# Edge lists of a gated graph layer: marks made by ScalarE, masked copies by GpSimd, fewer VectorE operations

## The chip, the core and the metric

The kernel runs on one core of a Trainium2 chip. The engines are PE (TensorE, with its weight loads shown as PEld), DVE (VectorE), ACT (ScalarE), POOL (GpSimd) and SP (SyncE, here only a DMA queue). The metric is device microseconds of one execution; the time of a kernel is the median of its runs.

## The reference

One layer of a graph network with a gate on every edge. `x` is 16 batches of 1024 vertices with 256 features, `adj` a 1024x1024 matrix that is nonzero in about 0.8% of its places, the diagonal among them.

```python
pre_u  = einsum('bud,dk->buk', h, W1[:d])
pre_v  = einsum('bvd,dk->bvk', h, W1[d:])
hidden = relu(pre_u[:, :, None, :] + pre_v[:, None, :, :] + b1)
S   = sigmoid(einsum('buvk,ko->buvo', hidden, W2)[..., 0] + b2[0])
a_t = einsum('buv,bud->bvd', S * A, h)
m_t = einsum('uv,bud->bvd', A, h) * h
out = beta1*h + beta2*(a_t @ Wa + ba) + beta3*(m_t @ Wm + bm)
```

Only places where `A` is nonzero count, so the kernel works on lists of edges.

## The kernel before

**Tiling.** The target vertices v are cut into 8 blocks of 128 (`NT`), the batches into 4 groups of 4 (`NG`, `GB`). A block has two halves of 64 vertices (`W`), and each half a list of up to 640 edges, that is 5 tiles (`TW`) of 128 edge slots. A block of one batch group is thus 10 steps (`T`), and the whole kernel 320 steps. The blocks 0 to 5 come first for groups 0 and 1, then 6 and 7, then all blocks for groups 2 and 3.

**A step.** POOL gathers 128 rows of 2048 numbers from a table in DRAM that holds (h W1u | h) of each source vertex, by the indices `uidx` (L528, into 8 buffers, the gather slots). PE expands the block's h W1v to the edges with a 0/1 matrix `mark` (L627, into two PSUM buffers `pc`, issued two steps ahead). DVE adds both (L657) and takes the product with W2 under the relu, for each of 4 batches (L664, four SCALAR_TENSOR_TENSOR with a sum). ACT makes the sigmoid and the gated 0/1 columns `left` (L667, L635, L671), and PE adds up the gathered h by target vertex (L680, `acc`), which makes the gather slot free again. Around them lie the table's own matmuls (L426) and the closing products of each block (L743).

**The lists.** `lists(vt)` (from L226) makes the lists of block vt. DVE turns the row of `adj` into keys, and ACT counts them (L239); DVE draws the 24 largest keys of each row (L245 and on) and how many were drawn (`used`). A product with a triangular matrix on PE (L275) and a maximum (L281) give `first`, the slot where each row's edges begin, and two operations give `held`, how many it gets. Then DVE makes the 128x640 mark: a 1 in row u at each slot from `first` to `first + held`. It is made in two passes: L294 tests slot < first + held, L301 tests slot >= first and multiplies. A small tile `R` holds for each row: held, first, the row's number times N, a one, `inw`, and the 24 keys (29 columns, `RC`). DVE multiplies it by the flags `soon` and `late` (row below 64, or not) into the two copies of `RR` (L312). POOL casts the mark to bytes (`few`, L314) and stores them with four DMAs (L317). PE multiplies mark and RR (L320, ten matmuls), so that each slot gets the values of its row; ACT copies that to `L` (L324), and DVE works out from L the slot's key, the indices `uidx` and `vidx` and the one-hot columns (L328 to L351). POOL fetches the values of `adj` by `vidx` (L360, 10 fetches per list).

**The order of the work.** Every engine runs its instructions in program order (`manual_schedule`), and the program is written in that order by generators. The lists of blocks 0 to 3 (`EARLY`) are made in the startup, in an order given by a table of strings. The lists of blocks 4 to 7 are started at steps 7, 14, 44 and 82 and have to be done by step 110. `fill` takes one piece of a list (up to the next `yield "op"`) ahead of each of the four gates L664 of a step; a `yield "slot"` or `"step"` goes on one step later, a `"wait"` two. A list with fewer DVE pieces therefore reaches each later piece in an earlier step. At step 120 POOL takes the largest remainder over all rows (L949), for a fallback that handles edges that found no slot.

Of the kernel before, what the change touches and what calls it, by code (L numbers as in the profile page):

```python
# [17 lines left out]
def kernel(  # L18
# [42 lines left out]
    nc = tc.nc  # L61
    B, N, D = x.shape
    NT = N // P
# [13 lines left out]
    RC = 5 + S  # L77
# [23 lines left out]
    def fixed(shape, name, dt=FP):  # L101
        return const.tile(shape, dt, name=name)
# [9 lines left out]
    upto = fixed([P, E], "upto")  # L112
# [7 lines left out]
    late = fixed([P, 1], "late")  # L120
    nc.vector.tensor_scalar(late, row, float(W), None, ALU.is_ge)
    soon = fixed([P, 1], "soon")
    nc.vector.tensor_scalar(soon, row, float(W), None, ALU.is_lt)


    inw = fixed([P, 1], "inw")
# [5 lines left out]
    reached = fixed([P, TW], "reached")  # L132
# [14 lines left out]

    slot, nth = fixed([P, E], "slot"), upto[:, :S]
    for j in range(TW):
        for half in range(2):  # L150
            nc.gpsimd.tensor_copy(
                slot[:, j * P + half * W:j * P + half * W + W].rearrange("p (e f g) -> p e f g", e=2, f=8),
                upto[:, j * P:(j + 1) * P].rearrange("p (e g half f) -> p half e f g", e=2, g=4, half=2)[:, half ^ j % 2])
# [11 lines left out]


    unit = fixed([P, P], "unit", FR)
    nc.vector.tensor_scalar(unit, upto[:, :P], 0.0, None, ALU.is_ge)
# [16 lines left out]
    thr = const.tile([P, NT], FP, name="thr")  # L185
    rest = const.tile([P, NT], FP, name="rest")
    nc.gpsimd.memset(val, 0.0)

# [8 lines left out]
    lst = ExitStack()  # L197
# [26 lines left out]


    def lists(vt):  # L226
        key = fetched[vt + 1][:, :N] if vt < EARLY else lst.tile([P, N], FP, name="key", bufs=1)
        (nc.sync if vt < EARLY else nc.gpsimd).dma_start(key, adjT[vt * P:(vt + 1) * P, :])
        yield "load"
        R = lst.tile([P, RC], FP, name="R", bufs=4)  # L230
        top = R[:, 5:5 + S]
        count = lst.tile([P, 1], FP, name="count", bufs=4)
        unread = whose[:, vt * NW:(vt + 1) * NW, :].rearrange("p w e -> p (w e)")[:, :N]
# [4 lines left out]
        yield "slot"  # L238
        nc.scalar.activation(unread, key, AF.Sign, accum_out=count)  # L239
        yield "cut"  # L240
# [20 lines left out]

        used = lst.tile([P, S], FP, name="used", bufs=4)
        nc.vector.tensor_scalar(used, top, 0.0, None, ALU.is_gt, ALU.add, accum_out=R[:, 0:1])
# [8 lines left out]
        nc.vector.tensor_scalar(ahead_, reached, R[:, 0:1], None, ALU.mult)  # L272
# [4 lines left out]
        first = R[:, 1:2]  # L277
        from_ = lst.tile([P, TW], FP, name="from", bufs=4)
        nc.vector.tensor_tensor(from_, pw[:, :TW], start_, ALU.add)
        yield "op"  # L280
        nc.vector.tensor_reduce(first, from_, AX.X, ALU.max)  # L281
        yield "op"

        held = lst.tile([P, 1], FP, name="held", bufs=4)
        nc.vector.tensor_scalar(held, first, -1.0, until, ALU.mult, ALU.add)
        yield "op"
        nc.vector.tensor_scalar(held, held, 0.0, R[:, 0:1], ALU.max, ALU.min)
        yield "op"
        nc.vector.tensor_tensor(R[:, 0:1], held, first, ALU.add)
        yield "op"  # L290
        nc.vector.tensor_tensor(rest[:, vt:vt + 1], count, held, ALU.subtract)
        yield "cut"
        mark = lst.tile([P, E], FP, name="made", bufs=1)
        nc.vector.tensor_scalar(mark, slot, R[:, 0:1], None, ALU.is_lt)  # L294
        yield "op"
        none = lst.tile([P, 1], FP, name="none", bufs=4)
        nc.vector.tensor_scalar(none, held, 0.0, float(N + 1), ALU.is_equal, ALU.mult)
        yield "op"
        nc.vector.tensor_scalar(held, held, -1.0, None, ALU.add)
        yield "op"  # L300
        nc.vector.scalar_tensor_tensor(mark, slot, first, mark, ALU.is_ge, ALU.mult)  # L301
        yield "op"
        last = lst.tile([P, 1], FP, name="last", bufs=4)
        nc.vector.scalar_tensor_tensor(used, nth, held, top, ALU.is_equal, ALU.mult, accum_out=last)
        yield "op"
        nc.vector.tensor_tensor(thr[:, vt:vt + 1], last, none, ALU.add)
        yield "op"
        RR = lst.tile([P, NW, RC], FP, name="RR", bufs=2)
        few = lst.tile([P, E], mybir.dt.uint8, name="few", bufs=2)
        yield "slot"  # L310
        for w, mine in enumerate((soon, late)):
            nc.vector.tensor_scalar(RR[:, w, :], R, mine, None, ALU.mult)  # L312
        yield "step"
        nc.gpsimd.tensor_copy(few, mark)  # L314
        for w in range(NW):
# [3 lines left out]
        for j in range(TW):  # L319
# [7 lines left out]
        s_of = lst.tile([P, M], FP, name="s_of", bufs=2)  # L327
        nc.vector.tensor_tensor(s_of, slot_of.rearrange("p w j -> p (w j)"), L[:, :, 1], ALU.subtract)  # L328
        yield "op"
# [3 lines left out]
        yield "op"  # L333
        nc.vector.tensor_tensor(eq, eq, L[:, :, 5:], ALU.mult)
        yield "op"
# [5 lines left out]
        yield "op"  # L341
        nc.vector.tensor_tensor(k_of, L[:, :, 2], k_of, ALU.subtract)
        yield "op"
        nc.vector.scalar_tensor_tensor(k_of, L[:, :, 3], -BIG, k_of, ALU.mult, ALU.add)
        yield "op"
        nc.vector.tensor_scalar(vidx[:, sl].rearrange("p w j -> p (w j)"), k_of, BIG + N, None, ALU.add)
        yield "op"
# [4 lines left out]
            onehot[:, sl], place.unsqueeze(1).to_broadcast([P, NW, TW, V]),  # L352
            col[:, :, :, 4:5].to_broadcast([P, NW, TW, V]), ALU.is_equal)

# [540 lines left out]
    for n in range(total + 2):  # L895
# [45 lines left out]
        if n == LISTS:  # L941
# [5 lines left out]
            nc.vector.tensor_scalar(minus[0], ident, -1.0, None, ALU.mult)  # L947
        if n == 120:
            nc.gpsimd.partition_all_reduce(longest, rest, P, bass_isa.ReduceOp.max)  # L949
            after(n + 12, count_rest)  # L950
# [115 lines left out]
```

## Time and profile before

| | |
|---|---|
| median of 3 runs | 1043.19 us (1042.17 to 1044.06) |
| profiled execution | 1040.67 us, span 1038.9 us, mean clock 0.984 |
| PE busy | 956.6 us (92%) |
| DVE busy | 965.1 us (93%) |
| ACT busy | 866.3 us (83%) |
| POOL busy | 465.6 us (45%) |

The busy time of an engine is the time in which it had an instruction of its own running; waiting, and the issue of DMAs by POOL's sequencer, are not counted apart from what their rows show. A row of the timeline gives start, duration, engine, line, operation, output and inputs. A row of the stretches gives the window, its length, the busy time of PE, PEld, DVE, ACT and POOL with the number of instructions, the mean clock that PE was granted, the busy share of the DMA engines, and GB/s.

### The profile page before, as it was taken

Reading aid. Unit: us, or ns where it says so; the run is one execution under the profiler, and the core shown is the slowest. Engines: PE = TensorE matmul, PEld = TensorE weight load, DVE = VectorE, ACT = ScalarE, POOL = GpSimd, SP = SyncE. Lnnn points to the kernel's source line nnn. Section 1 sums busy time; section 2 is a strip of 40 time slices with the busy share of each in tenths; the row PEclk is TensorE's granted clock in tenths of the full one; section 3 lists DMA queues with packets and bytes.
Section 4 is the critical chain, followed back from the end, with each engine's and each line's share of the span. In section 5 each row is a group of like instructions: output and inputs, shape, how many; then the busy total and the mean of one; then the engine's idle time right before and its main releaser. Section 6 shows DMA issues by size and latency. Waiting matters only on the chain.

```text
span 1038.9 us, 21679 instructions
## 1 busy us (share of the span) xinstructions
PE 956.6 (92%) x6393; PEld 699.2 (67%) x6393; DVE 965.1 (93%) x3388; ACT 866.3 (83%) x2722; POOL 465.6 (45%) x481
## 2 busy tenths in 40 slices
PE   7776899898888999999999899999999999999986
PEld 6653666675566766776777677777777777766753
DVE  8768999987999999999999799999999999999992
ACT  3335779787788988898999799999999999999972
POOL 4765675646256433573432333433434444444420
PEclk9878999999999999999999999999999999999999
DMA  9999999999899999999999999999999999999981
GB/s 286 336 366 363 338 354 334 342 327 384 294 338 347 348 414 362 385 367 412 407 409 404 383 412 406 390 406 403 403 373 384 380 367 361 376 375 368 378 325 34
DMA packets 133119, 375.01 MB, mean 361 GB/s; under 512 B 17680, under 2 KB 87824, under 8 KB 96784
## 3 DMA queue, kind: packets, MB, share of 16 engines
q0 software_dynamic: 50544, 301.16, 75.2%
q1 hardware_dynamic: 81824, 71.85, 21.5%
q8 instruction: 53, 0.87, 0.3%
q10 hardware_dynamic: 624, 0.52, 0.2%
q14 instruction: 74, 0.61, 0.2%
HBM read 377.53 MB, written 50.33 MB: 412 GB/s over the span
## 4 chain that ended last, share of the span: by engine, by line
PE 43%; DVE 36%; issue 10%; DMA 5%; ACT 4%; POOL 1%; another core or an unknown queue 0%; DVEq 0%; POOLq 0%; ACTq 0%
DVE fetched L664 17%; DVE fetched L657 12%; PE misc L426 12%; PE misc L743 9%; PE pc L627 8%; PE acc L680 7%; DMA fetched<-table,uidx 5%; PE misc L702 3%; DVE LT L719 2%; ACT left L671 1%; PE misc L739 1%; DVE low L489 1%; PE misc L430 1%; PE misc L777 1%; DVE cand L245 1%
## 5 line engine op out<-in xcount | busy, mean ns | idle before, releaser
L528 POOL DMA_INDIRECT fetched<-table,uidx x320 | 344.0, 1075 | 484.8 <-PE acc L680 340.0
L664 DVE SCALAR_TENSOR_TENSOR fetched<-fetched,w_b 128x256 f32<-128x256 f32 x1280 | 474.7, 415 | 0.0
L657 DVE TENSOR_TENSOR fetched<-fetched,pc 128x1024 f32<-128x1024 f32 x320 | 387.2, 1210 | 40.1 <-DMA fetched<-table,uidx 13.8
L671 ACT ACTIVATE left<-left,gt 128x16 f32<-128x16 f32 x1280 | 285.7, 298 | 0.0
L627 PE MATMUL pc<-X,mark 128*128 128x512 f32 x640 | 228.5, 451 | 33.8 <-DVE fetched L657 29.3
L680 PE MATMUL acc<-fetched,left 128*32 128x256 f32 x2560 | 186.2, 388 | 12.3 <-issue 4.9
L627 PEld LDWEIGHTS pc<-X,mark 128*128 128x128 f32 x640 | 105.8, 190 | 123.6 <-DVE fetched L657 52.7
L667 ACT ACTIVATE gt<-sc,b_b 128x4 f32<-128x4 f32 x320 | 96.8, 302 | 47.4 <-DVE fetched L664 41.2
L680 PEld LDWEIGHTS acc<-fetched,left 128*32 128x32 f32 x2560 | 73.4, 109 | 90.1 <-issue 28.0
L426 PE MATMUL misc<-w_u,hT 128*128 128x256 f32 x512 | 124.7, 391 | 6.6 <-DMA hT<-in_xT_dram 6.0
L426 PE MATMUL misc<-w_v,hT 128*128 128x256 f32 x512 | 122.6, 383 | 0.0
L743 PE MATMUL misc<-w_a,LT 128*128 128x256 f32 x496 | 117.5, 379 | 2.8 <-ACT LT L439 1.9
L743 PE MATMUL misc<-w_m,LT 128*128 128x256 f32 x496 | 118.7, 383 | 0.0
L426 PEld LDWEIGHTS misc<-w_u,hT 128*128 128x128 f32 x512 | 99.5, 196 | 24.0 <-DMA w_u<-in_W_dram 6.0
L426 PEld LDWEIGHTS misc<-w_v,hT 128*128 128x128 f32 x512 | 98.2, 192 | 15.9
L743 PEld LDWEIGHTS misc<-w_a,LT 128*128 128x128 f32 x496 | 93.8, 190 | 18.1 <-ACT LT L439 2.5
L688 ACT COPY ev<-acc 128x512 f32<-128x512 f32 x160 | 92.4, 577 | 16.2 <-PE misc L426 5.8
L635 ACT ACTIVATE left<-onehot,val 128x32 f32<-128x32 bf16 x320 | 100.1, 313 | 0.0
L360 POOL DMA_INDIRECT val<-in_adjT_dram,vidx x80 | 85.0, 1063 | 31.8 <-issue 20.8
L664 DVE DVE_READ_ACCUMULATOR fetched<-fetched,w_b 128x1 f32 x1280 | 97.8, 76 | 0.0
L743 PEld LDWEIGHTS misc<-w_m,LT 128*128 128x128 f32 x496 | 90.2, 192 | 9.9
L702 PE MATMUL misc<-ident,ev 128*128 128x128 f32 x642 | 83.2, 274 | 9.0 <-issue 3.1
(148 smaller groups left out, 885.4 us busy)
## 6 DMA issues: line engine op xcount, KB each, us to landing
hT<-in_xT_dram SPq DMA_DIRECT2D x35, 512.0 KB
table<-in_x_dram SPq DMA_DIRECT2D x32, 512.0 KB
out_dram<-z SPq DMA_DIRECT2D x62, 256.0 KB
table<-tab SPq DMA_DIRECT2D x48, 256.0 KB
fetched<-table,uidx POOLq DMA_INDIRECT x320
table<-fetched SPq DMA_DIRECT2D x8, 512.0 KB
fetched<-in_adjT_dram SPq DMA_DIRECT2D x4, 512.0 KB
key<-in_adjT_dram POOLq DMA_DIRECT2D x4, 512.0 KB
```

The costliest lines, as they stand in the source:

```text
L426: nc.tensor.matmul(p[:, bb * D:(bb + 1) * D], hT[:, 2 * h + bb, i, :], wt[:, i, :], start=(i == 0 and not begun), stop=(i == DC - 1), skip ...
L528: nc.gpsimd.indirect_dma_start(out=fetched[at_slot[n]], out_offset=None, in_=table[g], in_offset=bass.IndirectOffsetOnAxis(ap=uidx[:, vt * ...
L627: nc.tensor.matmul(pcs[n][:, c], marks[n // TW][:, j * P:(j + 1) * P], cuts[k][w][:, c], start=True, stop=True)
L635: nc.scalar.activation(lefts[n][:, 1::GB, :], onehot[:, vt * NW + w, j, :].unsqueeze(1).to_broadcast([P, GB // 2, V]), AF.Copy, scale=val[ ...
L657: nc.vector.tensor_tensor(t, t, pcs.pop(n), ALU.add)
L664: nc.vector.scalar_tensor_tensor(t[:, b, :], t[:, b, :], 0.0, w2_b, ALU.max, ALU.mult, accum_out=sc[:, b:b + 1])
L667: nc.scalar.activation(gt, sc, AF.Sigmoid, bias=b2_b)
L671: nc.scalar.activation(lefts[n][:, 2 * b, :], lefts[n][:, 1 + b // 2 * GB, :], AF.Copy, scale=gt[:, b:b + 1])
L680: nc.tensor.matmul(accs[i][b * 2 * V:(b + 1) * 2 * V, r, :], left[:, 2 * b - b % 2:2 * b - b % 2 + 2].rearrange("p k v -> p (k v)"), f[:, ...
L688: nc.scalar.copy(evs[i], accs.pop(i))
L702: nc.tensor.matmul(pt[:, :, FROM[j]:FROM[j] + V], evs[i][:, r, c * P:(c + 1) * P], ident, is_transpose=True, start=(j == of[0]), stop=True ...
L743: nc.tensor.matmul(pz[:, bb * D:(bb + 1) * D], LT[:, 2 * h + bb, i if bb else 1 - i, c, :], wt[:, c, :], start=(i == 1 and bb == 0 and c = ...
```

## The change

What it does, for each list:

- The mark is made by ACT from the distance to the middle of the row's slots. DVE writes two numbers, `span` = (held/2, −held/2 − first), and ACT computes relu(sign(held/2 − |slot + 1/2 − first − held/2|)), three dependent operations on 128x640 in place.
- The masked copies RR are made by POOL in one multiplication with a two-column tile `sides`, directly ahead of `few`. It used to be two DVE operations, a step ahead of it.
- Three columns of R (the row's number, `inw`, a constant) are the same for every list. They are written once into four tiles R, which are allocated once and used again. R has 28 columns instead of 29; the block's share of the row's number is added as a constant in the last step to `vidx`.
- `start_` is added by a second PE matmul (the identity, 128x5) into the same PSUM tile instead of by DVE.
- The threshold `thr` is one DVE operation over 25 columns of R, the first of which is the constant N + 1. It was four operations.
- ACT writes its count into `rest`, DVE leaves `held` in `taken`, and one subtraction at step 120 stands ahead of POOL's reduction.

DVE loses fourteen instructions per list and gets two. At the start, POOL writes the constant columns (4 copies) and adds 0.5 to `slot` (128x640), the latter with a switch of its library. The tile of the mark has one buffer and `few` two, as before.

The line numbers move: L320 is L314 in the changed kernel, L324 is L318, L314 is L308, L317 is L311, L528 is L520, L627 is L619, L680 is L672; new are L301 to L303 (ACT) and L306 (POOL).

On POOL, in the startup, from the first list's cast to the first gather (`val` are the value fetches, `whose` the stored marks, `fetched` a gather). Before:

```order
L314 CAST few<-made 128x640
L317 DMA whose<-few 64x640 x4
L360 DMA val<-in_adjT_dram,vidx 128x1 x10
L314 CAST few<-made 128x640
L317 DMA whose<-few 64x640 x4
L360 DMA val<-in_adjT_dram,vidx 128x1 x3
L314 CAST few<-made 128x640
L317 DMA whose<-few 64x640 x4
L528 DMA fetched_177<-table_60,uidx 128x2048
```

After, on the same engine at the same place:

```order
L306 TENSOR_TENSOR RR<-R_193,sides 128x56
L308 CAST few<-made 128x640
L311 DMA whose<-few 64x640 x4
L352 DMA val<-in_adjT_dram,vidx 128x1 x10
L306 TENSOR_TENSOR RR<-R_194,sides 128x56
L308 CAST few<-made 128x640
L311 DMA whose<-few 64x640 x4
L352 DMA val<-in_adjT_dram,vidx 128x1 x3
L306 TENSOR_TENSOR RR<-R_195,sides 128x56
L308 CAST few<-made 128x640
L311 DMA whose<-few 64x640 x4
L520 DMA fetched_182<-table_60,uidx 128x2048
```

RR now stands in POOL's queue ahead of each cast; for the second list it stands behind ten fetches, for the third behind three.

On PE, at the product of the last list, with the semaphores that an instruction waits for (Activation is ACT, DMASW a gather). Before:

```order
L680 MATMUL acc<-fetched_182,left 32x256 [waits DMASW6_49,Activation_49]
L680 MATMUL acc<-fetched_182,left 32x256 [waits Activation_49] x3
L627 MATMUL pc<-X,mark 128x512 [waits DVE_49]
L627 MATMUL pc<-X,mark 128x512
L320 MATMUL misc<-RR,made 128x58 [waits PE_49,Activation_49]
L320 MATMUL misc<-RR,made 128x58 x4
L627 MATMUL pc<-X,mark 128x512 [waits DVE_49]
```

After:

```order
L672 MATMUL acc<-fetched_185,left 32x256 [waits DMASW4_49,Activation_49]
L672 MATMUL acc<-fetched_185,left 32x256 [waits Activation_49] x3
L619 MATMUL pc<-X,mark 128x512 [waits DVE_49]
L619 MATMUL pc<-X,mark 128x512
L314 MATMUL misc<-RR,made 128x56 [waits Activation_49,Pool_49]
L314 MATMUL misc<-RR,made 128x56 x4
L619 MATMUL pc<-X,mark 128x512 [waits DVE_49]
```

The product stands at the same place among accumulates and expands, but it waits for ACT (the mark) and POOL (RR), and the expands of the next steps stand behind it.

The diff, cut to its core:

```diff
+    sides = fixed([P, NW], "sides")
+    nc.vector.tensor_scalar(sides[:, 0:1], row, float(W), None, ALU.is_lt)
+    nc.vector.tensor_scalar(sides[:, 1:2], row, float(W), None, ALU.is_ge)
...
+    nc.gpsimd.tensor_scalar(slot, slot, 0.5, None, ALU.add)
...
+    Rs = [lst.tile([P, RC], FP, name=f"R{i}") for i in range(EARLY)]
+    for R in Rs:
+        nc.gpsimd.tensor_copy(R[:, 1:4], known)
...
-        nc.vector.tensor_scalar(R[:, 2:3], row, float(N), float(vt * P * N), ALU.mult, ALU.add)
-        yield "op"
-        nc.vector.memset(R[:, 3:4], 1.0)
-        yield "op"
-        nc.vector.tensor_copy(R[:, 4:5], inw)
...
-        nc.tensor.matmul(pw[:, :TW], before, ahead_, start=True, stop=True)
+        nc.tensor.matmul(pw[:, :TW], before, ahead_, start=True, stop=False)
+        nc.tensor.matmul(pw[:, :TW], ident, start_, start=False, stop=True)
...
-        nc.vector.tensor_tensor(R[:, 0:1], held, first, ALU.add)
-        yield "op"
-        nc.vector.tensor_tensor(rest[:, vt:vt + 1], count, held, ALU.subtract)
+        nc.vector.tensor_scalar(span[:, 0:1], held, 0.5, None, ALU.mult)
+        yield "op"
+        nc.vector.scalar_tensor_tensor(span[:, 1:2], held, -0.5, first, ALU.mult, ALU.subtract)
         yield "cut"
+        nc.vector.scalar_tensor_tensor(used, upto[:, :S + 1], held, R[:, 3:], ALU.is_equal, ALU.mult,
+                                       accum_out=thr[:, vt:vt + 1])
         mark = lst.tile([P, E], FP, name="made", bufs=1)
-        nc.vector.tensor_scalar(mark, slot, R[:, 0:1], None, ALU.is_lt)
...
-        nc.vector.scalar_tensor_tensor(mark, slot, first, mark, ALU.is_ge, ALU.mult)
...
         yield "slot"
-        for w, mine in enumerate((soon, late)):
-            nc.vector.tensor_scalar(RR[:, w, :], R, mine, None, ALU.mult)
+        nc.scalar.activation(mark, slot, AF.Abs, bias=span[:, 1:2])
+        nc.scalar.activation(mark, mark, AF.Sign, bias=span[:, 0:1], scale=-1.0)
+        nc.scalar.activation(mark, mark, AF.Relu)
         yield "step"
+        RR = lst.tile([P, NW, RC], FP, name="RR", bufs=2)
+        nc.gpsimd.tensor_tensor(RR, R.unsqueeze(1).to_broadcast([P, NW, RC]), sides.unsqueeze(2).to_broadcast([P, NW, RC]),
+                                ALU.mult)
         nc.gpsimd.tensor_copy(few, mark)
...
+            nc.vector.tensor_tensor(rest, rest, taken, ALU.subtract)
             nc.gpsimd.partition_all_reduce(longest, rest, P, bass_isa.ReduceOp.max)
```

More of the change, by code (lines that the diff above doesn't have):

```diff
@@ L148 @@
     slot, nth = fixed([P, E], "slot"), upto[:, :S]
+    known = fixed([P, 3], "known")
+    nc.vector.tensor_scalar(known[:, 0:1], row, float(N), -BIG, ALU.mult, ALU.add)
+    nc.gpsimd.tensor_copy(known[:, 1:2], inw)
+    nc.gpsimd.memset(known[:, 2:3], float(N + 1))
     for j in range(TW):
@@ L276, in lists @@
+        nc.tensor.matmul(pw[:, :TW], ident, start_, start=False, stop=True)
         yield "wait"
-        first = R[:, 1:2]
-        from_ = lst.tile([P, TW], FP, name="from", bufs=4)
-        nc.vector.tensor_tensor(from_, pw[:, :TW], start_, ALU.add)
+        first = R[:, 0:1]
+        nc.vector.tensor_reduce(first, pw[:, :TW], AX.X, ALU.max)
         yield "op"
-        nc.vector.tensor_reduce(first, from_, AX.X, ALU.max)
-        yield "op"
-        held = lst.tile([P, 1], FP, name="held", bufs=4)
+        held = taken[:, vt:vt + 1]
@@ L299, in lists @@
[L299 to L308, printed above, removed]
```

41 lines of the change are left out of this document (17 added, 24 removed).

## The prediction

> **What bounds the kernel now.** I read the page first: the span, the busy time of the engines, the shares of the chain that ended last, and two groups, PE's expand and the add that takes it (busy time, mean ns, idle time ahead and what ended most of it).
>
> ```profile
> span 1038.9 us, 21679 instructions
> PE 956.6 (92%) x6393; PEld 699.2 (67%) x6393; DVE 965.1 (93%) x3388; ACT 866.3 (83%) x2722; POOL 465.6 (45%) x481
> PE 43%; DVE 36%; issue 10%; DMA 5%; ACT 4%; POOL 1%; another core or an unknown queue 0%; DVEq 0%; POOLq 0%; ACTq 0%
> L627 PE MATMUL pc<-X,mark 128*128 128x512 f32 x640 | 228.5, 451 | 33.8 <-DVE fetched L657 29.3
> L657 DVE TENSOR_TENSOR fetched<-fetched,pc 128x1024 f32<-128x1024 f32 x320 | 387.2, 1210 | 40.1 <-DMA fetched<-table,uidx 13.8
> ```
>
> TensorE and VectorE share the bound: 92% and 93% busy, 43% and 36% of the chain. The lists that the change edits are built in the startup and in some 365 us after it, so I asked for the stretches from 100 to 465 us: length, busy time of PE, PEld, DVE, ACT and POOL with their instructions, granted clock, DMA share, GB/s.
>
> ```profile
> 100.00:125.00 25.00, 20.89 (x122) 13.50 (x122) 20.85 (x80) 19.21 (x63) 16.72 (x17) 1.00 0.98 326
> 300.00:400.00 100.00, 93.84 (x624) 68.40 (x623) 95.67 (x333) 87.14 (x271) 47.11 (x48) 0.98 0.99 362
> sum 365.00, PE 333.84 PEld 241.27 DVE 340.39 ACT 304.63 POOL 196.87; mean PE 47.69 PEld 34.47 DVE 48.63 ACT 43.52 POOL 28.12
> ```
>
> In these 365 us PE is idle for 365 − 333.84 = 31.2 us and DVE for 365 − 340.39 = 24.6. Neither is full. A microsecond taken from DVE here is worth at most a microsecond, and a microsecond of PE waiting costs about as much. The question is which of the two the change moves more.
>
> **The change: what DVE loses.** Per list, fourteen DVE instructions go and two come. Their price is the distance from one instruction to the next, since on this engine they overlap. The timeline of DVE (start, duration, instruction) shows one of each kind:
>
> ```profile
> 191.53 0.15 DVE L291 TENSOR_TENSOR rest<-count,held 128x1 f32<-128x1 f32 x1
> 191.60 0.42 DVE L664 SCALAR_TENSOR_TENSOR fetched<-fetched,w_b 128x256 f32<-128x256 f32 x1
> 191.94 0.55 DVE L294 TENSOR_SCALAR made<-slot,R 128x640 f32<-128x640 f32 x1
> 192.41 0.42 DVE L664 SCALAR_TENSOR_TENSOR fetched<-fetched,w_b 128x256 f32<-128x256 f32 x1
> 195.90 0.87 DVE L301 SCALAR_TENSOR_TENSOR made<-slot,R,made 128x640 f32<-128x640 f32 x1
> 196.70 0.41 DVE L664 SCALAR_TENSOR_TENSOR fetched<-fetched,w_b 128x256 f32<-128x256 f32 x1
> 201.02 0.23 DVE L312 TENSOR_SCALAR RR<-R,soon 128x29 f32<-128x29 f32 x1
> 201.17 0.23 DVE L312 TENSOR_SCALAR RR<-R,late 128x29 f32<-128x29 f32 x1
> ```
>
> A small one costs 191.60 − 191.53 = 0.07 us, L294 0.47, L301 0.80, the two masked copies 0.15 each. Ten small ones go and two come: −8 × 0.07 = −0.56. With L294, L301 and 2 × 0.15 it is −0.56 − 0.47 − 0.80 − 0.30 = −2.13 us per list. The threshold over 25 columns for 24 is nothing I can price apart from a small one. Four lists run in the loop: −8.5. The first of them runs from about 100 us, where DVE has 20.85 of 25.00 us busy and PE 20.89, so what DVE saves there becomes waiting; I credit the other three, −6.4. The four lists of the startup are chained through other engines (below), and I credit nothing for them.
>
> **What PE gains as a wait.** The product of the marks (PE, L320 before, L314 after) used to need only what DVE had written a step earlier. Now it needs the mark from ACT and the masked copy RR from POOL, and RR stands in POOL's queue directly ahead of the cast "few", behind gathers that wait for PE itself. The best price for "when does POOL reach that place" is when it reached "few". The four products of the loop on PE, and the four casts on POOL:
>
> ```profile
> 148.15 1.22 PE L320 MATMUL misc<-RR,made 128*128 128x58 f32 x10
> 207.44 1.22 PE L320 MATMUL misc<-RR,made 128*128 128x58 f32 x10
> 297.74 1.22 PE L320 MATMUL misc<-RR,made 128*128 128x58 f32 x10
> 417.67 1.22 PE L320 MATMUL misc<-RR,made 128*128 128x58 f32 x10
> ```
>
> ```profile
> 154.57 0.90 POOL L314 CAST few<-made 128x640 uint8<-128x640 f32 x1
> 205.45 0.72 POOL L314 CAST few<-made 128x640 uint8<-128x640 f32 x1
> 300.50 0.72 POOL L314 CAST few<-made 128x640 uint8<-128x640 f32 x1
> 419.55 1.20 POOL L314 CAST few<-made 128x640 uint8<-128x640 f32 x1
> 417.04 0.99 POOL L528 DMA_INDIRECT fetched<-table,uidx  x1 [4.70 <-PE acc L680]
> ```
>
> RR itself has no row. Its nearest are a POOL copy of 128x64 and, as an upper end, the cast of 128x640; I take 0.4 us, since 56 columns lie by the first:
>
> ```profile
> L151 POOL COPY slot<-upto 128x64 f32<-128x64 f32 x10 | 2.5, 304 | 0.0
> L560 ACT CAST mark<-whose 128x640 fp32r<-128x640 uint8 x64 | 46.3, 723 | 0.0
> ```
>
> So the waits would be 154.57 + 0.4 − 148.15 = 6.8 us; none for the second list, whose cast is ahead of its product; 300.50 + 0.4 − 297.74 = 3.2; 419.55 + 0.4 − 417.67 = 2.3. Together 12.3. With fewer DVE pieces the lists finish two or three steps sooner and meet other gathers, so a single wait may move; the last gather above shows the kind of place, 4.70 us behind PE's acc. While PE stands at L314, its later expands (L619) and accumulates (L672) stand behind it, and with them DVE's adds, ACT's L318 and the gather slots.
>
> A stand of PE can cost again. Windows of 3.40 us, with the clock in the column ahead of the DMA share:
>
> ```profile
> 329.50:332.90 3.40, 1.16 (x7) 0.79 (x7) 3.40 (x11) 2.73 (x8) 2.03 (x2) 1.00 1.03 353
> 332.90:336.30 3.40, 3.40 (x10) 2.68 (x9) 2.52 (x9) 3.38 (x12) 2.48 (x4) 0.51 0.76 290
> 469.50:472.90 3.40, 1.63 (x19) 0.61 (x18) 2.98 (x11) 3.18 (x10) 2.11 (x2) 1.00 1.02 414
> 472.90:476.30 3.40, 3.40 (x20) 3.01 (x21) 3.40 (x14) 1.98 (x8) 0.37 (x1) 1.00 1.02 420
> ```
>
> With 1.16 us of work in a window, the next has half the clock (0.51), and 1.7 us of PE's work in it is lost; with 1.63 us it keeps it. A wait of about 2 us is enough, so I charge three: 3 × 1.7 = 5.1. PE then loses 12.3 + 5.1 = 17.4 us. The Trainium skill, "TensorE: Matmul & The Clock Gate", section "HAM oscillation — how this bites in real kernels", has it milder: “The abstract rule is "no PE-idle gaps >~3.4µs."” By it only the first of the waits would cost clock; the row with 1.16 of 3.40 busy, thus 2.24 us idle, and half the clock behind it, speaks against that.
>
> How much of 17.4 ends on the path? PE is 333.84/365 = 91% busy there; two pc buffers let it stand a step ahead of DVE, and eight gather slots lie between it and the transfers. Bounds are nothing and all; I take half, +8.7, as PE and DVE share the chain nearly evenly.
>
> **The rest in the loop.** ACT takes three operations of 128x640 per list, by the cast above 0.72 each, 2.2 us per list; ACT is idle 60 us of the 365 (304.63 busy), and the mark is made a step ahead of its product: nothing, or up to 2.2 where ACT's gates stand behind. PE's second matmul into the same PSUM: five columns, under 0.1. The subtract of rest and taken at step 120 is one small DVE operation; the reduction on POOL behind it then waits for DVE.
>
> **The startup.** RR of list 1 now stands behind the ten value fetches of list 0, and the product of list 1 waits for it. POOL's fetches (first and last) and its first gather, then PE's product of list 1, ACT's copy of it, DVE's first add that follows the gathers:
>
> ```profile
> 29.15 1.10 POOL L360 DMA_INDIRECT val<-in_adjT_dram,vidx  x1 [6.60 <-DVE onehot L351]
> 42.16 0.99 POOL L360 DMA_INDIRECT val<-in_adjT_dram,vidx  x1 [0.30 <-issue]
> 53.93 1.07 POOL L528 DMA_INDIRECT fetched<-table,uidx  x1 [0.33 <-issue]
> 38.29 1.22 PE L320 MATMUL pc<-RR,made 128*128 128x58 f32 x10
> 43.17 0.40 ACT L324 COPY L<-pc 128x290 f32<-128x290 f32 x1 [1.60 <-remote]
> 63.44 1.22 DVE L657 TENSOR_TENSOR fetched<-fetched,pc 128x1024 f32<-128x1024 f32 x1 [1.84 <-issue]
> 50.00:75.00 25.00, 18.99 (x70) 14.31 (x71) 16.45 (x64) 8.86 (x22) 16.72 (x21) 0.73 1.06 361
> ```
>
> The fetches end at 43.15; RR to 43.6; product to 44.8; the copy starts there and not at 43.17, 1.6 later; list 2 has its own RR on POOL, 0.4. So the first gather goes from 53.93 to about 55.9, +2.0. As the DMA engines are full in that stretch (1.06) with transfers that have to be made anyway, half of it shows: +1.0. The edits ahead of it (kept columns, slot + 0.5, and a library switch of POOL for that operation) lie in POOL's 6.60 us of waiting for DVE. The one switch of before is no dearer than the gap between these two:
>
> ```profile
> 472.96 0.37 POOL L949 PARTITION_ALL_REDUCE longest<-rest  x1 [0.21 <-issue]
> 477.55 1.03 POOL L528 DMA_INDIRECT fetched<-table,uidx  x1 [4.22 <-PE acc L680]
> ```
>
> Sum: −6.4 + 8.7 + 1.0 = +3.3 us.
>
> **The rivals.** *PE's waits are hidden* (faster). PE's expands wait 29.3 us in all for DVE's adds in the row of the expand, so PE often stands ahead of DVE; if it does so by more than some 3 us at three of the products, the waits only replace those waits. Then −6.4 + 1.0 = −5.4, 1035.3 on the profiled execution, and with the fourth list's 2.1 down to −7.5. Against it: PE was idle for only 31 us in 365, and the gather slots wait for its acc.
>
> *The clock holds* (same). If no window at the waits falls short enough, PE loses 12.3, half of it 6.2: −6.4 + 6.2 + 1.0 = +0.8. It is also what the milder rule of the Trainium skill's page would come near to: with one loss of 1.7 for three, by halves, +1.6.
>
> *The transfers decide* (same). The DMA share is 0.99 from 300 to 400 us. If gathers set the pace, DVE's saving and PE's waits both vanish into waiting for them: the startup's +1.0 is left. Against it: of 40.1 us that L657 waits, 13.8 at most are laid to a gather.
>
> *The startup slips* (slower). If PE, waiting for RR of list 1, drops to half clock, the products and the table's matmuls behind it take twice as long; PE is 18.99 of 25.00 busy there. 5 us lost at the first gather, with nothing hiding them, stand in place of 1.0: +3.3 + 4.0 = +7.3; with three quarters of 17.4 instead of half, 4.4 more, +11.7. It decides from about 5 us at the first gather.
>
> **How the numbers follow.** The profiled execution took 1040.67 us, 1.8 more than its span, and 2.5 less than the median of the three runs, 1043.2. I add the sum to the median: 1043.2 + 3.3 = 1046.5. Chances: forecast 0.32; waits hidden 0.31 (about 1037.8); clock holds 0.14 (1044.0); transfers decide 0.13 (1044.2); startup 0.10 (1050 to 1055). A measurement of this kernel can tell 0.2%, 2.1 us, from no change: faster 0.31, same 0.27, slower 0.42. The range holds the hidden waits' value at its low end and the near half of the startup's at its high end: 1037 to 1052. The forecast's own, with a quarter to three quarters of 17.4 on the path, is 1042 to 1051.
>
> **What would show it.** On PE, idle time ahead of L314 of 2 to 7 us at three of the four loop lists, released by POOL's RR; windows at half clock behind them; DVE's busy time from 100 to 465 us some 8 us lower, and its waits on pc higher; the first gather near 56. The forecast is wrong if PE hardly waits at L314 or DVE's adds don't start later behind such a wait (then faster), or if the first add comes later than 68 us.

## The result and the profile after

The changed kernel took 1057.78 us (median of 4 runs, 1051.87 to 1063.67) beside 1042.68 us for the kernel before (4 runs, 1039.82 to 1044.06): 1.0146 times the time, 95% interval 1.0104 to 1.0188. A second comparison gave 1.0114 (1.0086 to 1.0141). The sign was forecast; the size, 15 us, lies outside the range. The profiled execution took 1058.45 us.

The page of the changed kernel: span, busy time, the chain that ended last, and DVE's add.

```profile
span 1056.7 us, 21672 instructions
PE 973.5 (92%) x6409; PEld 712.4 (67%) x6409; DVE 950.4 (90%) x3294; ACT 884.6 (84%) x2746; POOL 469.0 (44%) x496
PE 53%; DVE 25%; issue 10%; ACT 5%; DMA 4%; POOL 3%; another core or an unknown queue 0%; POOLq 0%; DVEq 0%
L649 DVE TENSOR_TENSOR fetched<-fetched,pc 128x1024 f32<-128x1024 f32 x320 | 388.0, 1213 | 55.6 <-PE pc L619 29.7
```

DVE did 14.7 us less work (965.1 to 950.4), as the edit wanted, and its add waited 15.5 us longer (40.1 to 55.6); the largest part of the wait is now for PE's expand (29.7), where it was for a gather (13.8). PE's share of the chain rose from 43% to 53%, which fits a saving made on the engine that was not the tighter one.

Next, PE's first rows of the four loop products (start, duration, and in brackets the idle time ahead with its releaser), then POOL's multiplications that release them.

```profile
150.91 1.32 PE L314 MATMUL misc<-RR,made 128*128 128x56 f32 x5 [5.47 <-POOL RR L306]
207.64 1.63 PE L314 MATMUL misc<-RR,made 128*128 128x56 f32 x8 [2.87 <-POOL RR L306]
306.59 1.81 PE L314 MATMUL misc<-RR,made 128*128 128x56 f32 x9 [2.04 <-POOL RR L306]
425.58 1.58 PE L314 MATMUL misc<-RR,made 128*128 128x56 f32 x10 [1.98 <-POOL RR L306]
```

```profile
150.56 0.29 POOL L306 TENSOR_TENSOR RR<-R,sides 128x56 f32<-128x56 f32 x1
207.28 0.30 POOL L306 TENSOR_TENSOR RR<-R,sides 128x56 f32<-128x56 f32 x1
306.25 0.29 POOL L306 TENSOR_TENSOR RR<-R,sides 128x56 f32<-128x56 f32 x1
425.23 0.29 POOL L306 TENSOR_TENSOR RR<-R,sides 128x56 f32<-128x56 f32 x1
```

All four waits end some 0.35 us after RR starts. They sum to 12.36 us. RR itself takes 0.29. What it stands behind shows at the third list: two gathers, the first of which waited for PE.

```profile
303.76 0.99 POOL L520 DMA_INDIRECT fetched<-table,uidx  x1 [3.44 <-PE acc L672]
305.06 1.16 POOL L520 DMA_INDIRECT fetched<-table,uidx  x1 [0.30 <-issue]
306.25 0.29 POOL L306 TENSOR_TENSOR RR<-R,sides 128x56 f32<-128x56 f32 x1
```

The fourth list has the same picture (3.67 for PE). Ahead of the first list's RR, gathers and value fetches follow each other with 1.3 to 1.7 us from start to start, and of the last four only one waited for PE (1.35).

RR comes last, but it is not alone. ACT's mark is late as well. This is the last of its three operations at each of the four lists:

```profile
147.38 0.74 ACT L303 ACTIVATE made<-made 128x640 f32<-128x640 f32 x1
205.05 0.74 ACT L303 ACTIVATE made<-made 128x640 f32<-128x640 f32 x1
303.63 0.74 ACT L303 ACTIVATE made<-made 128x640 f32<-128x640 f32 x1
424.15 0.74 ACT L303 ACTIVATE made<-made 128x640 f32<-128x640 f32 x1
```

PE became free at 145.44, 204.77, 304.55 and 423.60 (start of the product less the wait). With RR ready it would still have waited for the mark for some 2.7, 1.0, 0 and 1.3 us: 5.0 of the 12.36. RR alone accounts for the other 7.4.

What follows the first of them shows in windows of 3.40 us (PE, PEld, DVE, ACT, POOL busy; clock; DMA share; GB/s), and in the one row of DVE behind it:

```profile
148.40:151.80 3.40, 0.89 (x4) 0.90 (x5) 3.40 (x9) 2.01 (x8) 2.78 (x4) 0.74 0.88 279
151.80:155.20 3.40, 3.40 (x12) 3.04 (x13) 0.01 (x2) 0.39 (x1) 2.19 (x4) 0.50 0.79 250
155.20:158.60 3.40, 3.40 (x13) 2.69 (x12) 0.00 (x0) 0.59 (x1) 0.00 (x0) 0.76 0.16 53
```

```profile
160.54 1.22 DVE L649 TENSOR_TENSOR fetched<-fetched,pc 128x1024 f32<-128x1024 f32 x1 [8.73 <-PE pc L619]
```

One stand of PE goes through three stages here. PE stands, the others go on. Then PE is back, but the clock is at 0.74, 0.50 and 0.76 in the three windows, together 3.4 us of it lost (some 0.4 before PE was back), while DVE and ACT have next to nothing to do. Then, as no accumulate has freed a gather slot, the DMA engines run dry, at 0.16. DVE stood 8.73 us for a wait of 5.47.

### The profile page after: what moved, and what is told of

Its sections match the earlier page's. It is cut to its first block, busy times and chain, and to the rows that moved or that the text cites. A ratio compares the mean times of both kernels' runs of the same rounds, so it can differ in the third digit from the quotient of the medians.

```text
span 1056.7 us, 21672 instructions
## 1 busy us (share of the span) xinstructions
PE 973.5 (92%) x6409; PEld 712.4 (67%) x6409; DVE 950.4 (90%) x3294; ACT 884.6 (84%) x2746; POOL 469.0 (44%) x496
## 4 chain that ended last, share of the span: by engine, by line
PE 53%; DVE 25%; issue 10%; ACT 5%; DMA 4%; POOL 3%; another core or an unknown queue 0%; POOLq 0%; DVEq 0%
PE misc L418 15%; DVE fetched L656 13%; PE misc L735 11%; PE pc L619 10%; DVE fetched L649 10%; PE acc L672 8%; PE misc L694 4%; DMA fetched<-table,uidx 2%; DMA hT<-in_xT_dram 2%; POOL fetched L520 2%; PE misc L731 2%; ACT left L663 1%; DVE LT L711 1%; PE misc L314 1%; PE misc L422 1%
## 5 line engine op out<-in xcount | busy, mean ns | idle before, releaser
L520 POOL DMA_INDIRECT fetched<-table,uidx x320 | 342.5, 1070 | 491.8 <-PE acc L672 349.3
L649 DVE TENSOR_TENSOR fetched<-fetched,pc 128x1024 f32<-128x1024 f32 x320 | 388.0, 1213 | 55.6 <-PE pc L619 29.7
L619 PE MATMUL pc<-X,mark 128*128 128x512 f32 x640 | 231.0, 455 | 22.9 <-DVE fetched L649 18.4
L672 PE MATMUL acc<-fetched,left 128*32 128x256 f32 x2560 | 187.0, 390 | 7.7 <-ACT ev L680 5.6
L619 PEld LDWEIGHTS pc<-X,mark 128*128 128x128 f32 x640 | 107.4, 192 | 112.2 <-issue 52.1
L418 PE MATMUL misc<-w_u,hT 128*128 128x256 f32 x512 | 129.1, 402 | 8.2 <-DMA hT<-in_xT_dram 5.8
L672 PEld LDWEIGHTS acc<-fetched,left 128*32 128x32 f32 x2560 | 73.1, 109 | 86.2 <-issue 24.0
L735 PE MATMUL misc<-w_a,LT 128*128 128x256 f32 x496 | 120.2, 385 | 2.3 <-ACT LT L431 1.3
L418 PEld LDWEIGHTS misc<-w_u,hT 128*128 128x128 f32 x512 | 102.5, 202 | 26.2 <-DMA w_u<-in_W_dram 5.7
L680 ACT COPY ev<-acc 128x512 f32<-128x512 f32 x160 | 92.3, 577 | 16.0 <-PE acc L672 4.9
L656 DVE DVE_READ_ACCUMULATOR fetched<-fetched,w_b 128x1 f32 x1280 | 100.7, 79 | 0.0
L627 ACT ACTIVATE left<-onehot,val 128x32 f32<-128x32 bf16 x320 | 99.9, 312 | 0.0
```

The costliest lines, as they stand in the source:

```text
L418: nc.tensor.matmul(p[:, bb * D:(bb + 1) * D], hT[:, 2 * h + bb, i, :], wt[:, i, :], start=(i == 0 and not begun), stop=(i == DC - 1), skip ...
L520: nc.gpsimd.indirect_dma_start(out=fetched[at_slot[n]], out_offset=None, in_=table[g], in_offset=bass.IndirectOffsetOnAxis(ap=uidx[:, vt * ...
L619: nc.tensor.matmul(pcs[n][:, c], marks[n // TW][:, j * P:(j + 1) * P], cuts[k][w][:, c], start=True, stop=True)
L627: nc.scalar.activation(lefts[n][:, 1::GB, :], onehot[:, vt * NW + w, j, :].unsqueeze(1).to_broadcast([P, GB // 2, V]), AF.Copy, scale=val[ ...
L649: nc.vector.tensor_tensor(t, t, pcs.pop(n), ALU.add)
L656: nc.vector.scalar_tensor_tensor(t[:, b, :], t[:, b, :], 0.0, w2_b, ALU.max, ALU.mult, accum_out=sc[:, b:b + 1])
```

## The experiments

The theory (1): RR's place in POOL's queue, behind gathers (some of which wait for PE) and value fetches, makes PE stand at the product; the half clock and the slots behind it make the loss. Rivals: (2) ACT's three operations delay its gates and copies; (3) the startup slipped. Each ratio is against the kernel before in the same comparison, whose own medians were 1037.0, 1037.4, 1025.0 and 1024.8 us in the four; so between comparisons the ratios can be compared, not the times.

**RR back on DVE.** In the changed kernel, one piece ahead of the step of the product:

```diff
+        for w in range(NW):
+            nc.vector.tensor_scalar(RR[:, w, :], R, sides[:, w:w + 1], None, ALU.mult)
         yield "step"
-        nc.gpsimd.tensor_tensor(RR, R..., sides..., ALU.mult)
```

> The changed kernel with the masked copies RR back on VectorE, one piece ahead of the step of the product; ScalarE's marks and the rest as changed. Theory 1 (PE's waits for GpSimd's RR, 12.4 us at the four loop products, make the loss): those waits go, the time falls to 1036 to 1042 us. Theory 2 (ScalarE's three operations per list delay its gates and copies): still 1052 to 1058. Theory 3 (the startup, whose first add came 3.3 us later, and what follows from it): 1050 to 1056.

1044.98 us, 1.0069 (1.0040 to 1.0099). Over half of the loss is gone, though not all that theory 1 had expected. PE's waits at the loop products fell to 2.75, 0.88, 0.83 and 1.34 us, and none is for POOL any more. The first, second and last end within 0.1 us of the end of ACT's mark (147.97, 201.82 and 412.15 in this trace).

**Marks back on DVE**, RR still on POOL:

```diff
-        nc.scalar.activation(mark, slot, AF.Abs, bias=span[:, 1:2])
-        nc.scalar.activation(mark, mark, AF.Sign, bias=span[:, 0:1], scale=-1.0)
-        nc.scalar.activation(mark, mark, AF.Relu)
+        nc.vector.tensor_scalar(mark, slot, end_, None, ALU.is_lt)
+        nc.vector.scalar_tensor_tensor(mark, slot, first, mark, ALU.is_ge, ALU.mult)
```

> The changed kernel with the marks back on VectorE (two operations on 128x640 per list), RR still on GpSimd. Theory 1: PE still waits for RR, 1055 to 1062 us. Theory 2: near the kernel before, 1040 to 1046. Theory 3: 1050 to 1058, as the library switch and GpSimd's queue of the startup are unchanged.

1058.01 us, 1.0204 (1.0149 to 1.0258). Rival 2 falls as the main cause: without ACT's marks the loss is all there. The ratio is above the changed kernel's 1.0146 and 1.0114; since these were not in one comparison, it stays open whether the marks on ACT gain something.

**Both back on DVE**, the other edits kept:

> The changed kernel with marks and RR back on VectorE; the constant columns, PE's second matmul and the one-operation threshold stay, nine VectorE operations per list fewer than before. Theories 1 and 2: 1040 to 1043 us, the kernel before or a little under. Theory 3: 1046 to 1050.

1040.44 us, 1.0031 (1.0000 to 1.0062). In time this lies in the range of theory 1; as a ratio it is a little over the kernel before, where a gain of DVE's work had been hoped for.

**RR alone on POOL**, in the kernel before:

> The kernel before with the one edit that RR is made by GpSimd, directly ahead of its cast. Theory 1: PE waits at the product as in the changed kernel, 1053 to 1060 us. Theory 2 and theory 3: within 3 us of the kernel before, 1040 to 1046.

1058.93 us, 1.0207 (1.0149 to 1.0264). One edit of 0.3 us per list makes a loss at least as large as the whole change's. It brings something else along, which is shown further down: POOL switches its library ahead of the first RR and again ahead of the reduction (9.10 and 8.49 us of idle time there in this trace). So this run does not separate the place in the queue from the switches.

**RR earlier in POOL's queue.** The same instruction, same engine, moved to right behind the maximum that completes R:

```diff
         nc.vector.tensor_reduce(first, pw[:, :TW], AX.X, ALU.max)
+        RR = lst.tile([P, NW, RC], FP, name="RR", bufs=2)
+        nc.gpsimd.tensor_tensor(RR, R..., sides..., ALU.mult)
         yield "op"
```

> The changed kernel with GpSimd's RR issued right after the maximum that completes R, so that in the loop it stands ahead of the two gathers that it stood behind; the same instruction, the same engine, only its place in GpSimd's queue. If the place in the queue is what costs (theory 1): PE's wait at the loop products falls under 1 us where the mark is ready, and the time comes near that of the kernel with RR on VectorE, 1041 to 1047 us. Rival, GpSimd's instruction itself or its sharing with VectorE costs: 1052 to 1060.

1041.18 us, 1.0033 (1.0012 to 1.0053). The library switches are still there, so the place in the queue makes most of the loss. The rival, that POOL's instruction itself costs, falls. The group of the loop's products in the changed kernel and then here (each with the last product of the startup, 3.1 and 3.9 us of the wait):

```profile
L314 PE MATMUL misc<-RR,made 128*128 128x56 f32 x50 | 10.4, 383 | 15.4 <-POOL RR L306 15.4
```

```profile
L314 PE MATMUL misc<-RR,made 128*128 128x56 f32 x50 | 8.6, 335 | 10.0 <-POOL RR L285 3.9 <-issue 3.5 <-ACT made L306 2.6
```

What POOL still releases here is the startup's; in the loop nothing waits for RR. Of the remaining 6.1 us, 5.2 end within 0.2 us of the end of ACT's mark. RR moved ahead in the startup too (the first add comes at 63.2 us, 66.7 in the changed kernel), so this run does not divide the loss between startup and loop.

**RR on POOL in the loop alone**, in the kernel before:

```diff
+        if vt < EARLY:
+            for w in range(NW):
+                nc.vector.tensor_scalar(RR[:, w, :], R, sides[:, w:w + 1], None, ALU.mult)
         yield "step"
+        if vt >= EARLY:
+            nc.gpsimd.tensor_tensor(RR, R..., sides..., ALU.mult)
```

> The kernel before with RR on GpSimd for the four lists of the loop alone; the four of the startup keep VectorE's. Theory 1 as the traces have it (the loop's waits and what follows): 14 to 20 us over the kernel before. Rival, the startup (PE idle for 3.7 and 4.0 us there, the first add 1.7 to 3.3 us later) carries a good part: 6 to 12 us over it.

1057.53 us, 1.0185 (1.0130 to 1.0240): about the number that theory 1 expected, but the run can't be read that way. POOL's rows at the first of its lists:

```profile
155.74 1.00 POOL L364 DMA_INDIRECT val<-in_adjT_dram,vidx  x1 [0.30 <-issue]
165.69 0.27 POOL L316 TENSOR_TENSOR RR<-R,sides 128x58 f32<-128x58 f32 x1 [8.95 <-issue]
```

POOL switches its library ahead of the first multiplication, for 8.95 us. In the changed kernel that switch lies in the startup; here it fell into the loop and PE stood 15.42 us at that product. The startup's share, rival 3, stays unmeasured by it. The traces tell something on it all the same. How many us later than in the kernel before the add of a step starts (steps counted from 0; one execution each, the last two columns from another comparison than the first two):

| step | kernel before | changed | rr_dve | both_dve |
|---|---|---|---|---|
| 0 | 63.44 | +3.3 | +0.3 | −0.1 |
| 20 | 138.39 | +2.8 | +3.0 | +3.3 |
| 25 | 158.14 | +10.0 | +6.0 | +1.4 |
| 50 | 241.93 | +17.4 | +7.1 | +1.7 |
| 110 | 435.42 | +12.8 | −1.4 | −2.8 |
| 319 | 1012.89 | +16.8 | +2.1 | −1.7 |

The slip of the first add by RR in the startup is no longer to be seen at step 20, where the two runs without it are as late. The changed kernel falls behind between the steps 20 and 50, with the first two products of the loop.

**PE kept busy while it would wait.** Twenty matmuls into the product's own tile, ahead of each loop product, which overwrites it:

```diff
         pe = aside(vt)
+        if vt >= EARLY:
+            for j in range(20):
+                nc.tensor.matmul(pe[:, :P], ident, before, start=True, stop=True)
```

> The changed kernel with twenty idle 128x128 matmuls on PE ahead of each of the four loop products, written into the product's own tile before it and overwritten by it (about 2.2 us of PE). If the half clock behind the waits is a large part of the loss (theory 1a): the windows at half clock at the products shrink and the time falls by 4 to 10 us against the changed kernel, 1048 to 1054. If the wait and the gather slots behind it are the loss (theory 1b): 1056 to 1063, no gain or a little loss.

1050.41 us, 1.0105 (1.0068 to 1.0143). In its own comparison there was no run of the changed kernel, and the second comparison of that, expected as follows, gave 1038.45 us, 1.0114 (1.0086 to 1.0141):

> The changed kernel itself once more, beside the versions of it on the same chip. From its first comparison, 1.0146 of the kernel before: 1.010 to 1.020, so 1048 to 1058 us where the kernel before takes 1037. If the six microseconds that the busy PE recovered are real, it stands above that run's 1.0105.

So this pair decided nothing, and it was repeated side by side further down.

**Without the slot shift on POOL.** Both back on DVE, and no library switch in the startup (`slot` stays without the half). It was run twice:

> Marks and RR on VectorE and the other edits of the change, as in the run both_dve, without the shift of the slot numbers by one half on GpSimd and its library switch. If that switch in the startup made the 3 us by which both_dve stood over the kernel before: level with the kernel before or up to 4 us under it. If not: 2 to 5 us over it, as both_dve.

> The run both_dve_plain once more with more rounds: marks and RR on VectorE, no shift, no library switch, nine VectorE operations per list fewer. If VectorE's saving of the small operations is worth its time where the loop waits for VectorE (9 times 0.07 us times 4, 2.5 us): 0.996 to 0.999 of the kernel before. If the loop's order hides it: 0.999 to 1.001.

0.9981 (0.9948 to 1.0014), then 0.9996 (0.9980 to 1.0012): no change. Nine DVE instructions fewer per list show no gain clear of noise; the 2.5 us that the prediction's price gives for four lists would be 0.9976.

**RR on DVE, marks on ACT, the shift on DVE**, so no library switch in the startup; then the same with ACT's three operations issued a step earlier:

```diff
+        nc.scalar.activation(mark, slot, AF.Abs, bias=span[:, 1:2])
+        nc.scalar.activation(mark, mark, AF.Sign, bias=span[:, 0:1], scale=-1.0)
+        nc.scalar.activation(mark, mark, AF.Relu)
         yield "slot"
-        (the same three)
```

> ScalarE's marks kept, RR on VectorE, the shift by one half on VectorE, so no library switch in the startup. If ScalarE's marks (PE waits of 2.7, 0.9, 0.8 and 1.3 us for them in the run rr_dve) are what is left of the loss: 1.004 to 1.008 of the kernel before, as rr_dve. If the library switch was: 0.998 to 1.001.

> The run rr_dve_shift_dve with ScalarE's three operations issued a step earlier, ahead of the step that they opened. If PE's waits for the mark are what is left: they fall under 0.5 us each and the time falls to 0.994 to 1.000 of the kernel before. If ScalarE's own time, in front of its gates, is the cost: no better than rr_dve_shift_dve, 1.003 to 1.008.

1.0014 (1.0000 to 1.0028) and 1.0018 (1.0008 to 1.0029). In the second, PE's products in the loop wait for 0.4 us in all:

```profile
L314 PE MATMUL misc<-RR,made 128*128 128x56 f32 x50 | 6.2, 271 | 0.4 <-ACT LT L907 0.4
```

Here DVE is spared all that the change spares it but RR, PE is not held, and the kernel is not faster than before. Taken with ACT's operations, DVE's saving is worth no time here. Whether ACT's own time eats it is not shown.

The first of these runs bears on a rival that the three theories leave out, the library switch. It differs from rr_dve in the shift alone, and 1.0069 became 1.0014. Likewise both_dve, 1.0031, became 0.9981 and 0.9996 without the switch. That is 3 to 6 us in each pair, but no pair stood in one comparison. So it is open how much of the loss, and of the 1.0033 of rr_early, is the switch's.

**The reduction moved behind the gathers.** POOL's library has to be switched again for the reduction of step 120. In the profiled execution of the changed kernel, POOL's rows of the switch in the startup and of the reduction (the kernel before had 0.21 us ahead of it):

```profile
17.22 1.84 POOL L171 TENSOR_SCALAR slot<-slot 128x640 f32<-128x640 f32 x1 [8.68 <-DVE taken L289]
...
499.16 1.42 POOL L942 PARTITION_ALL_REDUCE longest<-rest  x1 [6.76 <-issue]
```

```diff
-        if n == 120:
+        if n == 310:
...
-            after(n + 12, count_rest)
+            after(n + 6, count_rest)
```

> The changed kernel with the reduction over the rows (and the subtraction ahead of it) moved from step 120 to step 310, behind nearly all gathers. In the kernels that use GpSimd's library in the startup, 6.8 to 8.4 us stand ahead of that reduction with the gathers behind it, and steps 127 to 129 take 3 us more. If that is a real part of the loss: 3 to 6 us under the changed kernel (1.0114 and 1.0146 of the kernel before), so 1.006 to 1.009. If it is given back at step 157, where the kernel before waits 5 us for a gather: 1.011 to 1.015, as before.

1040.47 us, 1.0150 (1.0127 to 1.0173). Nothing gained. The three steps from step 127 (between DVE's adds in the trace) took 7.55 us instead of the changed kernel's 11.00, and step 160 (counted from 0, as in the table; the expectation calls the place step 157) gave it back, waiting for a gather:

```profile
579.01 1.22 DVE L649 TENSOR_TENSOR fetched<-fetched,pc 128x1024 f32<-128x1024 f32 x1 [5.78 <-DMA fetched<-table,uidx]
```

The kernel before has such a wait there too, 5.42 us; the changed kernel came late enough to have none.

The same with PE kept busy, on the same chip, and both on DVE with the reduction late:

> The run late_reduce with the twenty idle matmuls of kept_busy ahead of the four loop products. If half clock behind PE's waits is a part of the loss: 0.003 to 0.007 under late_reduce on the same chip. If only the waits and the gather slots are: level with late_reduce within 0.002.

> The run both_dve (marks and RR on VectorE, the slot shift on GpSimd with its library switch), with the reduction at step 310. If the switch costs through the reduction: from 1.003 down to 0.998 to 1.001 of the kernel before, the value without a switch. If the switch costs in the startup: still 1.002 to 1.005.

The first took 1038.77 us, 1.0126 (1.0104 to 1.0147), 1.7 us under late_reduce; the intervals overlap, and 0.0024 lies between the two values expected. The matmuls themselves took longer than meant; the stretch of the four loop lists in late_reduce, and the group of the extra matmuls and the stretch in this one:

```profile
100.00:465.00 365.00, 340.45 (x2239) 251.12 (x2239) 335.73 (x1186) 315.08 (x965) 201.50 (x201) 0.97 0.97 357
```

```profile
L315 PE MATMUL misc<-before,ident 128*128 128x128 f32 x160 | 18.6, 276 | 0.8 <-ACT low L483 0.8
```

```profile
100.00:465.00 365.00, 349.77 (x2400) 263.33 (x2392) 337.73 (x1187) 315.19 (x966) 201.64 (x201) 0.99 0.98 358
```

They held PE for 18.6 us. In late_reduce it had waited for RR in this group:

```profile
L314 PE MATMUL misc<-RR,made 128*128 128x56 f32 x50 | 9.8, 366 | 14.3 <-POOL RR L306 14.3
```

Of these 14.3 us, 3.6 belong to the last product of the startup, so 10.7 to the four of the loop. With the filler PE was held 8 us longer there, and the clock rose from 0.97 to 0.99. Added up from windows of 1 us, 12.0 us of clock are lost in that stretch without the filler and 3.4 with it, so 8.5 us came back. The time did not grow. That fits a clock that is worth about as much time as the hold: an inference from the balance, since a shorter filler was not tried. Both on DVE with the late reduction gave 1.0012 (0.9995 to 1.0028), between the values with and without the switch; it doesn't decide whether the switch costs a measurable time, and late_reduce showed no gain from moving the second one.

## Why the prediction was right in sign and wrong in size

Two terms of the sum failed. −6.4 for DVE was credited in full, and the runs show none of it. The clock behind PE's waits was charged at 5.1 us, and 12 us of it are lost. Of two things put at nothing, ACT's mark cost PE 5 us of waiting, and for the library switch it is open.

- **PE's waits: right.** Forecast 6.8, 0, 3.2 and 2.3 us, 12.3 in all; measured 5.47, 2.87, 2.04 and 1.98, 12.36. The single ones moved with the lists, as the working allowed; that the sum agrees to 0.1 us is partly luck, since the second was forecast at none. That the place in POOL's queue makes them last so long is shown by rr_early.
- **ACT's mark: put at nothing, wrong.** The working had the mark made a step ahead of its product. PE came to three of the four products before it, by 5.0 us together, and in rr_dve, where RR is ready, PE still waits for 5.8 us. Only issuing the three operations a step earlier took this away (mark_early, 0.4 us).
- **The clock: mis-sized.** The working charged one half window, 1.7 us, for each of three waits. The windows behind the first wait lose (0.26 + 0.50 + 0.24) × 3.4 = 3.4 us of clock. Over the stretch of 365 us the loss is in these rows, of the kernel before and of the changed one:

```profile
100.00:465.00 365.00, 333.84 (x2200) 241.27 (x2200) 340.39 (x1217) 304.63 (x946) 196.87 (x195) 0.99 0.98 352
```

```profile
100.00:465.00 365.00, 332.13 (x2116) 240.62 (x2116) 322.75 (x1132) 297.02 (x909) 189.47 (x192) 0.96 0.95 341
```

  0.03 × 365 = 11 us of PE, against 5.1. Windows of 1 us give it closer: 15.4 against 3.4 us, so 12.0 more, of which the four products have 3.4, 3.4, 3.4 and 1.7. The one row that showed half a clock had a single window of it, and that was taken as the length of the state. The length is not the same each time: in the second comparison's trace of the changed kernel the four products have 3.4, 1.7, 1.7 and 1.7.
- **DVE's saving of 6.4 us: failed.** It was credited in full. both_dve_again (the small operations, no gain) and mark_early (1.0018, PE's products hardly held) give nothing for it; for the mark's two operations that is shown only together with the three that ACT got in their place. It rested on "a microsecond taken from DVE here is worth at most a microsecond", and the most was taken.
- **Half of PE's loss shows: held, roughly.** With 12.4 + 12.0 = 24.4 us lost and none gained by DVE, half is 12.2. With 1 to 3 us of the startup's slip it comes to 13 to 15, and 15.1 was measured. This is a balance, not a measurement: the library switch could stand in it for the startup or for a part of PE's loss. In rr_early PE loses 6.1 us ahead of the loop's products and 5.8 us more clock than in the kernel before, and 0.0033, 3.4 us, is all that the time shows.
- **The startup: mechanism right, size low.** The first gather went to 57.39 us (forecast 55.9), and DVE's first add from 63.44 to 66.71, +3.3 where +1.0 was charged. In other runs of the same startup it came at 64.5 to 65.8, so 1 to 3 us. The ten fetches, as forecast, hold PE for 3.75 us at the product of list 1. One more cause shows in the trace: for list 2, POOL's cast waited 2.83 us for ACT's mark, and PE 3.56. At list 3 PE waited 3.07 us more for RR. How much of it reaches the end stays open; by the table above it does not show at step 20.
- **The library switch: misread.** The gap of 4.22 us behind the reduction was read as the upper end of a switch's price. It was a wait for PE; the kernel before pays no switch at that place. The two switches of the changed kernel stand ahead of their instructions, with 8.68 and 6.76 us. The first was hidden in the trace, as forecast: POOL's next cast still waited 4.19 us for ACT's mark. The second cost 11.00 − 7.54 = 3.5 us in the three steps from step 127 and was absorbed at step 160. Yet the runs with the switches stand 0.003 to 0.006 above those without, so that they cost nothing is not shown.
- **The rivals.** "PE's waits are hidden" fell: DVE's waits for the expand between 100 and 485 us (total, times, longest) grew from the kernel before to the changed one.

```profile
DVE fetched L657 <- PE pc L627: 8.0, 5, 4.6
```

```profile
DVE fetched L649 <- PE pc L619: 21.0, 10, 8.7
```

"The clock holds" fell: behind the waits of the last two products, 2.04 and 1.98 us, the changed kernel's windows show 0.50 and 0.69 of the clock.

```profile
308.80:312.20 3.40, 3.40 (x9) 2.67 (x9) 3.40 (x10) 3.40 (x13) 1.36 (x3) 0.50 0.94 366
427.80:431.20 3.40, 3.40 (x14) 2.76 (x14) 3.03 (x11) 1.34 (x7) 0.87 (x2) 0.69 1.03 416
```

The Trainium skill ("TensorE: Matmul & The Clock Gate", section "HAM oscillation — how this bites in real kernels") puts its rule at idle gaps over about 3.4 us; these gaps are shorter, so the trace does not agree. "The transfers decide" was right only at step 160, where they swallowed the reload. "The startup slips" is not shown: the first add came 3.3 us later, not 5.

No version here beat the kernel before: the best, both on DVE without the shift (0.9981 and 0.9996), is level with it.

## What to carry to other kernels

Before moving a cheap instruction to an idle engine, look at what stands ahead of it in that engine's queue and who waits for it: an operation of 0.29 us per list on GpSimd, placed behind gathers and fetches that take 1.3 us or more each and partly wait for TensorE, made most of a loss of 15 us; issued earlier in the same queue, it left a loss of 0.33%. Issue such an instruction as soon as its inputs exist, not where its result is used. Price a stand of TensorE with the clock behind it, and credit work taken from an engine only where its waits show that it is the tighter one.

## What the runs showed that had not been expected

- A GpSimd operation such as TENSOR_TENSOR or TENSOR_SCALAR with a constant, behind copies, memsets and DMAs, was preceded by a library switch of 8.68 and 8.95 us in the two rows above; the reduction over partitions after it by another of 6.76 us, which it did not have in a kernel with no such operation ahead (0.21). The profile lays the 8.68 to DVE, but in rr_dve the same instruction stands behind 8.76 us that the profile lays to no other engine.
- ACT's three operations took more than the 0.72 us that had been read from a cast:

```profile
L301 ACT ACTIVATE made<-slot,span 128x640 f32<-128x640 f32 x8 | 6.6, 831 | 2.6 <-DVE span L294 2.6
L302 ACT ACTIVATE made<-made,span 128x640 f32<-128x640 f32 x8 | 6.6, 828 | 0.3
L303 ACT ACTIVATE made<-made 128x640 f32<-128x640 f32 x8 | 5.9, 737 | 0.3
```

- After a stand of TensorE of 2 us or more, the reduced clock was spread over three windows of 3.4 us at the first three of the loop's products, with 3.4 us of clock lost at each, not 1.7; in another execution of the same kernel it was so at the first one alone.
